# Attention and mixture of experts on one core: the first unit's heads spread in two chunks by SyncE, the second chunk's normalization on ScalarE, and the last tokens finished by pieces

## The chip, the core and the metric

The kernel runs on one core of a Trainium2 chip. The metric is the device time of the program in microseconds (us). Before the change it is 2261.02 us, the median of three runs (2259.83 to 2262.47). The profile comes from one further execution with the hardware profiler on.

## The reference, cut to what matters

x has 8 sequences of 1024 tokens with 256 values each, all in float32. There are 16 heads of 16 values and 8 experts of 512 hidden values.

```python
x = x + layernorm(attention(layernorm(x), Wq, Wk, Wv, Wo))   # causal softmax attention
x = x + layernorm(moe(layernorm(x), ...))
# moe: logits = h @ router_weight.T + router_bias; the two best of softmax(logits)
#      each chosen expert: gate, up = split(h @ gate_up_proj[e] + bias)
#      act = (clip(up, -7, 7) + 1) * min(gate, 7) * sigmoid(1.702 * min(gate, 7))
#      out = sum of the two of weight * (act @ down_proj[e] + down_bias[e])
```

## The kernel before, in words

**Attention** works in 32 units: unit u is a sequence b and a group g of four heads. The projections give q and k as [channel, token] in the tiles `unq` and `unk`. For a unit, `spread(u)` (L607) copies the 16 rows of each of its four heads to partitions 0, 32, 64 and 96 of `qP` and `kP`, with DMAs that SyncE (SP) issues: four for q and four for k, each of 16 rows and all 1024 tokens. For unit 0 alone the four for k are issued by ScalarE (ACT) (L615).

A unit is then done in steps (`STEPS`, L627 to L639). `maxima_tiles` computes scores `sa` (L686) and their row maxima on VectorE (DVE); in the next unit's time `values_tiles` computes the transposed scores `sb` (L781), their exponentials on ScalarE and the weighted values `av` (L818). The first two steps of a unit read only the first 512 tokens of `qP` and `kP`; the third and the fourth read the second 512.

Everything else (layer norms, projections of later units, the output projection, the router) is cut into small pieces by generators with hand-written costs. `pump` hands such pieces out between the pairs of heads. The order of TensorE (PE), DVE, ACT and SP in the attention part is the order of the source; GpSimd (POOL) keeps it by `in_order`.

**The beginning** (`begin`, L449) loads x and the weights, computes the layer norm statistics of the first sequence's two chunks of 512 tokens, and applies them in `apply` (L469): of the four rows of tiles `n` of a chunk, ACT does n = 0 and 2 (L481), DVE does n = 1 and 3 (L392). Then, for each chunk t, `turn_x` transposes the normalized tokens on PE (`xps`, L436) and ACT copies them (L437); `project_chunk` multiplies by the q and k weights (`pjq`, `pjk`, L591) and ACT copies into `unq`, `unk` (L595). At the end `begin` puts memsets on POOL: `mx`, the two `vpad` tiles, and `qP` and `kP` of units 1 and 2 (L510 to L515). POOL has nothing else to do there, so it starts on them as soon as the second `rstd` (L380) is done.

After `begin` comes `spread(0)`, then the generator `others` (L518). Its first step issues, all on SP, the loads of the router's weights `rwr` (L521), the biases `gubr` (L523), four broadcasts `rbias` (L525) and a store of zeros. Its next four steps transpose the v and o weights (`wps_v`, `wps_o`, L443) with copies on ACT (L444); these run ahead of the loop over units. The step after those is handed out by the first `pump` in unit 0: it transposes `rwr` (`rps`, L537), and the next one `gubr` (`gubps`, L541). So on PE the order is: `xps`, `pjq`, `pjk` of chunk 1; `wps_v`, `wps_o`; four matmuls `sa` of the first step's first pair of heads; `rps`; `gubps`; `sa` of the second pair; values `vps` (L577), and so on.

**The experts** work on 71 tiles of 256 rows sorted by expert. Each tile's results are scattered to `ytd` in DRAM by two indirect DMAs of POOL (L1337). `both(t)` (L1347) finishes 512 tokens: it loads the attention result (`x1`, L1350) and the two expert results of each token (`yy`, 1 MB, L1354), combines them with the router's weights (ACT L1368, DVE L1373), takes statistics (L1377, L1378), `ve` (L1381), `rstd` on POOL (L1385), `shift` (L1390), normalizes on ACT (L1397), adds `x1` on DVE (L1402) and stores 512 KB (L1404). It is a generator too; its steps are placed between the matmuls of later tiles by `an_end` (L1428). The 16th group of tokens is ready only when all tiles are done, so its `both` runs alone at the very end (L1468).

Of the kernel before, what the change touches and what calls it, by code (L numbers as in the profile page):

```python
# [13 lines left out]
ALU = mybir.AluOpType  # L14
# [44 lines left out]
def attn_moe_kernel(  # L59
# [345 lines left out]
    with ExitStack() as attn:  # L405
# [43 lines left out]
        def begin():  # L449

            wr = {}
            for name, w, queue, tag in (
                ("q", wq, nc.sync, "avs"), ("k", wk, nc.sync, "avs"),
                ("v", wv, nc.scalar, "aT"), ("o", wo, nc.scalar, "aT"),
            ):
                wr[name] = ap2.tile([P, KT, D], F32, tag=tag, name=f"wr_{name}")
                queue.dma_start(out=wr[name], in_=w.rearrange("(t p) i -> p t i", p=P))
            xt = xs[0]
            xnTs[0] = ap0.tile([P, KT, S], F32, tag="xnT", name="xnT_0")
            steps = [ln_steps(xt[:, ts(t, NTB), :], NTB) for t in range(NC)]  # L460

            def all_of(gen):
                while True:
                    try:
                        next(gen)
                    except StopIteration as end:
                        return end.value

            def apply(t, mv, rstd):  # L469
                shift = small.tile([P, NTB], F32, tag="shift", name="shift")  # L470
                nc.vector.scalar_tensor_tensor(
                    shift, mv[:, :, 0:1].rearrange("p n c -> p (n c)"), -1.0, rstd,
                    ALU.mult, ALU.mult,
                )
                xn = ap3.tile([P, NTB, D], F32, tag="xn", name=f"xn_0_{t}")
                for n in range(NTB):
                    of = xt[:, t * NTB + n, :]
                    if n % 2:
                        ln_apply(xn[:, n, :], of, mv, rstd, n)
                    else:  # L480
                        nc.scalar.activation(  # L481
                            xn[:, n, :], of, AF.Identity,
                            bias=shift[:, n : n + 1], scale=rstd[:, n : n + 1],
                        )
                return xn

            for name in ("q", "k"):
                uns[0, 0, name] = ap0.tile(
                    [P, S], F32, tag=f"un{name}0", name=f"un{name}_0_0"
                )  # L490
            fill(0)
            got = all_of(steps[0])
            for kt in range(KT):
                weights("q", wr["q"], kt)
            for _ in range(NTB // 2):
                next(steps[1])
            xn = apply(0, *got)
            got = all_of(steps[1])
            for kt in range(KT):
                weights("k", wr["k"], kt)  # L500
            for kt in range(KT):
                turn_x(0, 0, xn, kt)
            xn = apply(1, *got)
            for t in range(NC):
                if t:
                    for kt in range(KT):
                        turn_x(0, t, xn, kt)
                for name in ("q", "k"):
                    project_chunk(0, 0, name, t)
            for mx in mxs:  # L510
                in_order(nc.gpsimd.memset(mx, NEG))
            for vp in vps:
                in_order(nc.gpsimd.memset(vp, 1.0))
            for i in range(1, NU):
                fill(i)  # L515
            return wr
# [71 lines left out]
        def project_chunk(b, g2, name, c):  # L588
            ps = ps_b.tile([P, QC], F32, tag="b", name=f"pj{name}_{b}_{g2}_{c}")
            for kt in range(KT):  # L590
                nc.tensor.matmul(  # L591
                    ps, lhsT=wT[name][:, kt, ts(g2, P)], rhs=xnTs[b][:, kt, ts(c, QC)],
                    start=(kt == 0), stop=(kt == KT - 1),
                )
            nc.scalar.copy(uns[b, g2, name][:, ts(c, QC)], ps)  # L595
# [8 lines left out]
                    yield piece(pe=1.75, act=0.6, after=0 if c else 1)  # L604
                    project_chunk(b, g2, name, c)

        def spread(u):  # L607

            b, g = divmod(u, NG)
            row = qPs[u % NU].rearrange("(h r) (a n s) -> h r a n s", r=HS, n=TN, s=D)  # L610
            for a in range(S // (TN * D) if u >= NU else 0):
                nc.sync.dma_start(out=row[:, DH, a], in_=zeros[:HG, :, :D])
            for name, dsts in (("q", qPs), ("k", kPs)):

                queue = nc.scalar if u == 0 and name == "k" else nc.sync  # L615
                for hh in range(HG):
                    queue.dma_start(
                        out=dsts[u % NU][ds(hh * HS, DH), :],
                        in_=uns[b, g // 2, name][ds((g % 2 * HG + hh) * DH, DH), :],
                    )  # L620


# [508 lines left out]
        with tc.manual_schedule(  # L1131
# [2 lines left out]
            free[0] = False  # L1134
            jobs = {}
            wr = begin()
            spread(0)
            more = start(due, others(wr))
            for _ in range(2 * KT):
                emit(due, more)  # L1140
# [203 lines left out]
        yield  # L1344


    def both(t):  # L1347

        x1 = ap2.tile([P, NTB, D], F32, tag="y", name=f"x1_{t}")
        nc.sync.dma_start(out=x1, in_=x1_dram[t])  # L1350
        yy = x_buffer(f"yy_{t}")[:, : NTB * TOPK * D].rearrange(
            "p (n r d) -> p n r d", n=NTB, r=TOPK
        )
        load = nc.sync.dma_start(  # L1354
            out=yy,
            in_=yt_dram[ds(t * TB * TOPK, TB * TOPK), :].rearrange(
                "(p n r) d -> p n r d", p=P, n=NTB
            ),
        )
        ahead_of(load, "yt")  # L1360
        yield
        acc = ap2.tile([P, NTB, D], F32, tag="xT", name=f"acc_{t}")
        st = small.tile([P, NTB, 6], F32, tag="st", name="st")
        mv = small.tile([P, NTB, 2], F32, tag="mv", name="mv")

        for n in range(NTB + 1):
            if n < NTB:
# [9 lines left out]
                nc.vector.bn_stats(st[:, m, :], acc[:, m, :])  # L1377
                nc.vector.bn_aggr(mv[:, m, :], st[:, m, :])  # L1378
            yield
        ve = small.tile([P, NTB], F32, tag="ve", name="ve")  # L1380
        nc.vector.tensor_scalar(  # L1381
            ve, mv[:, :, 1:2].rearrange("p n c -> p (n c)"), EPS, None, ALU.add
        )
        rstd = small.tile([P, NTB], F32, tag="rstd", name="rstd")
        in_order(nc.gpsimd.tensor_tensor(rstd, ve, nhalf, ALU.pow))  # L1385
        yield
        yield

        shift = small.tile([P, NTB], F32, tag="shift", name="shift")
        nc.vector.scalar_tensor_tensor(  # L1390
            shift, mv[:, :, 0:1].rearrange("p n c -> p (n c)"), -1.0, rstd, ALU.mult, ALU.mult
        )
        yield
        o = ap2.tile([P, NTB, D], F32, tag="aT", name=f"o_{t}")
        for n in range(NTB + 1):
            if n < NTB:
                nc.scalar.activation(  # L1397
                    o[:, n, :], acc[:, n, :], AF.Identity,
                    bias=shift[:, n : n + 1], scale=rstd[:, n : n + 1],
                )  # L1400
            if n:
                nc.vector.tensor_tensor(o[:, n - 1, :], o[:, n - 1, :], x1[:, n - 1, :], ALU.add)  # L1402
            yield
        nc.sync.dma_start(out=out_t[t], in_=o)  # L1404

    def tiles_for(r):

# [5 lines left out]
    with tc.manual_schedule(engines={engines.PE, engines.DVE, engines.Activation}):  # L1413
# [52 lines left out]
        for _ in behind:  # L1466
            pass
        for r in [*waiting, *range(ready, NT)]:  # L1468
            ends.append((0, both(routed[r])))
        while ends:  # L1470
            an_end(NTILES)
        free[0] = True
# [36 lines left out]
```

## Time and profile before

| what | value |
|---|---|
| median of three runs | 2261.02 us (2259.83 to 2262.47) |
| the profiled execution's own time | 2283.45 us |
| its span in the trace | 2281.7 us |
| PE busy | 2197.9 us, 96% of the span |
| DVE busy | 1634.9 us, 72% |
| ACT busy | 1091.0 us, 48% |
| POOL busy | 1067.7 us, 47% |
| mean granted TensorE clock | 0.979 |

The span is the trace's first to last event; what lies around it is 1.75 us. A line of the timeline gives start, duration, engine, source line, operation, output and inputs, sizes and count, and in brackets how long the engine had been idle and what ended that. SPq and ACTq are the DMA-issuing sides of SyncE and ScalarE. A line of the windows gives, for a stretch of time, the busy time and the number of instructions of PE, its weight loads, DVE, ACT and POOL, then the granted TensorE clock (1.00 is full), the DMA engines' share and GB/s.

### The profile page before, as it was taken

Reading aid. Unit: us, or ns where it says so; the run is one execution under the profiler, and the core shown is the slowest. Engines: PE = TensorE matmul, PEld = TensorE weight load, DVE = VectorE, ACT = ScalarE, POOL = GpSimd, SP = SyncE. Lnnn points to the kernel's source line nnn. Section 1 sums busy time; section 2 is a strip of 40 time slices with the busy share of each in tenths; the row PEclk is TensorE's granted clock in tenths of the full one; section 3 lists DMA queues with packets and bytes.
Section 4 is the critical chain, followed back from the end, with each engine's and each line's share of the span. In section 5 each row is a group of like instructions: output and inputs, shape, how many; then the busy total and the mean of one; then the engine's idle time right before and its main releaser. Section 6 shows DMA issues by size and latency. Waiting matters only on the chain.

```text
span 2281.7 us, 45149 instructions
## 1 busy us (share of the span) xinstructions
PE 2197.9 (96%) x16801; PEld 1374.6 (60%) x16801; DVE 1634.9 (72%) x3677; ACT 1091.0 (48%) x2181; POOL 1067.7 (47%) x1228
## 2 busy tenths in 40 slices
PE   7999999999999999999999999799999999999995
PEld 4444444544445445445545444577888888888884
DVE  4766777777767767877767786375557888887775
ACT  2466665566666666666656656331212323332222
POOL 3321462572573463464473364355444544554543
PEclk8899999999999999999999999899999999999998
DMA  3101102102101111111111121458567877878773
GB/s 80 34 7 39 25 16 55 41 20 48 43 26 32 49 36 30 48 30 39 48 29 35 34 57 35 153 189 252 197 204 267 274 264 254 276 250 277 246 247 111
DMA packets 149106, 251.05 MB, mean 110 GB/s; under 512 B 25920, under 2 KB 111832, under 8 KB 146840
## 3 DMA queue, kind: packets, MB, share of 16 engines
q1 hardware_dynamic: 134168, 210.86, 30.2%
q0 software_dynamic: 12960, 35.47, 4.3%
q8 instruction: 133, 2.18, 0.4%
q10 hardware_dynamic: 1760, 1.84, 0.4%
q14 instruction: 85, 0.70, 0.1%
HBM read 175.66 MB, written 55.68 MB: 101 GB/s over the span
## 4 chain that ended last, share of the span: by engine, by line
PE 83%; POOL 6%; DVE 5%; issue 3%; ACT 1%; DMA 1%; SPq 0%; POOLq 0%; ACTq 0%; DVEq 0%
PE sa L686 19%; PE gu L1296 19%; PE av L818 11%; PE dn L1327 10%; PE sb L781 7%; PE vps L577 3%; PE pjk L591 3%; PE pjq L591 3%; PE yps L877 2%; PE avt L849 1%; PE xtps L1280 1%; POOL pT L798 1%; PE aps L869 1%; POOL xsd L1044 1%; POOL xn L392 1%
## 5 line engine op out<-in xcount | busy, mean ns | idle before, releaser
L789 ACT ACTIVATE pT<-sb 128x512 f32<-128x512 f32 x1152 | 625.0, 595 | 433.8 <-PE sb L781 381.3
L781 PE MATMUL sb<-qP,kP 32*128 32x512 f32 (+3 forms) x3072 | 722.1, 528 | 4.0 <-ACT pT L789 2.6
L686 PE MATMUL sa<-kP,qP 32*128 32x512 f32 (+3 forms) x3072 | 665.3, 532 | 3.5 <-DVE mx L702 2.2
L1296 PE MATMUL gu<-xsT,wg 128*128 128x256 f32 x2272 | 520.2, 382 | 1.2 <-ACT xsT L1282 1.2
L1296 PEld LDWEIGHTS gu<-xsT,wg 128*128 128x128 f32 x2272 | 434.0, 191 | 61.5 <-ACT xsT L1282 1.5
L798 POOL TENSOR_SCALAR_AFFINE_SELECT pT<-pT 128x512 f32<-128x512 f32 x256 | 159.5, 639 | 580.9 <-ACT pT L789 573.9
L702 DVE TENSOR_REDUCE mx<-sa 128x2 f32<-128x1024 f32 x256 | 311.8, 1219 | 127.9 <-PE sb L781 116.3
L1307 ACT ACTIVATE sig<-gate 128x256 f32<-128x256 f32 x284 | 118.3, 416 | 570.7 <-DVE gate L1305 523.7
L686 PEld LDWEIGHTS sa<-kP,qP 32*128 32x128 f32 x3072 | 232.7, 187 | 195.3 <-issue 101.0
L818 PE MATMUL av<-pT,vpad 128*32 128x256 f32 (+1 forms) x5120 | 348.5, 369 | 1.5 <-DVE avs L829 0.9
L1312 POOL TENSOR_TENSOR sig<-sig,gate 128x256 f32<-128x256 f32 x284 | 213.6, 753 | 291.2 <-ACT sig L1307 288.3
L781 PEld LDWEIGHTS sb<-qP,kP 32*128 32x128 f32 x3072 | 309.5, 186 | 44.7 <-ACT pT L789 15.7
L1327 PE MATMUL dn<-wd,act 128*128 128x256 f32 x1136 | 274.5, 382 | 16.4 <-DVE act L1317 16.4
L818 PEld LDWEIGHTS av<-pT,vpad 128*32 128x32 f32 x5120 | 116.8, 109 | 286.4 <-issue 216.7
L1305 DVE TENSOR_SCALAR gate<-gu,bs 128x256 f32<-128x256 f32 x284 | 135.9, 479 | 168.0 <-PE gu L1296 148.8
L1327 PEld LDWEIGHTS dn<-wd,act 128*128 128x128 f32 x1136 | 209.5, 191 | 48.8 <-DVE act L1317 23.7
L696 DVE CUSTOM_DVE_ANT_0 sa<-sa,cmask 128x512 f32<-128x512 f32 x256 | 178.2, 698 | 61.8 <-PE sb L781 30.6
L1337 POOL DMA_INDIRECT ytd<-ys,places x142 | 142.8, 1006 | 125.0 <-DVE ys L1333 98.5
L1044 POOL DMA_INDIRECT xsd<-xn,slots x128 | 127.5, 996 | 95.9 <-DMA xn<-second 51.4
L1317 DVE SCALAR_TENSOR_TENSOR act<-up,sig 128x256 f32<-128x256 f32 x284 | 124.4, 438 | 24.9 <-POOL sig L1312 24.9
L711 DVE TENSOR_REDUCE mx<-sa 128x2 f32<-128x512 f32 x128 | 87.9, 687 | 72.1 <-PE sb L781 42.6
L1309 DVE TENSOR_SCALAR up<-gu,bs 128x256 f32<-128x256 f32 x284 | 134.7, 474 | 0.0
(198 smaller groups left out, 2395.0 us busy)
## 6 DMA issues: line engine op xcount, KB each, us to landing
wg<-_L_ffn_gate_up_proj_dram SPq DMA_DIRECT2D x71, 1024.0 KB
wd<-in_L_ffn_down_proj_dram SPq DMA_DIRECT2D x71, 512.0 KB
xs<-xsd SPq DMA_DIRECT2D x67, 257.0 KB
yy<-ytd SPq DMA_DIRECT2D x16, 1024.0 KB
bs<-biasd SPq DMA_DIRECT2D x71, 132.0 KB
x<-in_L_attn_x_dram SPq DMA_DIRECT2D x16, 512.0 KB
qP<-unq SPq DMA_DIRECT2D x128, 64.0 KB
x1d<-y SPq DMA_DIRECT2D x16, 512.0 KB
```

Source lines behind the costliest of these rows:

```text
L686: nc.tensor.matmul(ps[:, hh, ds(at, w)], lhsT=qP[r, ts(i, P)], rhs=kP[r, ds(c * QC, w)], start=True, stop=True,)
L696: nc.vector.tensor_tensor_reduce(out=ps[:, hh, :], in0=ps[:, hh, :], in1=cmask, scale=1.0, scalar=NEG, op0=ALU.add, op1=ALU.max, accum_out ...
L702: nc.vector.tensor_reduce(mx[:, heads, i, 2:3], ps, AX.X, ALU.max)
L781: nc.tensor.matmul(banks[hh][:, ds(at, QC - off)], lhsT=kP[r, ts(j, P)], rhs=qP[r, ds(c * QC + off, QC - off)], start=True, stop=True,)
L789: nc.scalar.activation(pT[:, 2 * pair + hh, :], banks[hh], AF.Exp)
L798: in_order(nc.gpsimd.affine_select(out=d, in_=d, compare_op=ALU.is_ge, fill=0.0, base=0, pattern=[[0, HG], [1, P]], channel_multiplier=-1,))
L818: nc.tensor.matmul(av[ds(hh * HS, HS), ds(off + a - at, z - a)], lhsT=vp[:, j, ds((g * HG + hh) * VS, HS)], rhs=pT[:, hh, a:z],  start=c n ...
L1044: put = nc.gpsimd.indirect_dma_start(out=xs_dram[:, :], out_offset=bass.IndirectOffsetOnAxis(ap=slots[:, t, r, n : n + 1], axis=0), in_=xn ...
L1296: nc.tensor.matmul(ps[:, half, :], lhsT=wg[:, kt, ds(half * FF + f * P, P)], rhs=xT[:, kt, :], start=(kt == 0), stop=(kt == KT - 1),)
L1312: in_order(nc.gpsimd.tensor_tensor(sg, sg, gt, ALU.mult))
L1327: nc.tensor.matmul(ps[:, n, :], lhsT=act[:, f, ts(n, P)], rhs=wd[:, f, :], start=(f == 0), stop=(f == FT - 1),)
L1337: put = nc.gpsimd.indirect_dma_start(out=yt_dram[:, :], out_offset=bass.IndirectOffsetOnAxis(ap=places[:, i, n : n + 1], axis=0), in_=y[:, ...
```

## The change

Four edits at two places.

1. In `apply`, DVE normalizes rows n = 1 and 3 only for chunk 0; for chunk 1 ACT does all four.
2. `spread` gets a range of tokens, `cols`. `begin` calls it for unit 0 after each chunk's projections with that chunk's 512 tokens, so unit 0 takes 16 DMAs of half the size in place of 8, all issued by SP; ACT issues none. The call after `begin` is gone, so the loads of `others` stand on SP behind all 16.
3. `both` for the last 512 tokens (`final`) loads `yy` by four DMAs, one for each n, and no longer takes part in the ordering exception `ahead_of`, which lets later scatters pass a load.
4. In that `both`, `ve`, `rstd`, `shift`, the normalization, the addition and the store are done for two rows at a time. For all other tokens one piece of four remains, in the order of before.

```diff
                 for n in range(NTB):
                     of = xt[:, t * NTB + n, :]
-                    if n % 2:
+                    if n % 2 and t == 0:
                         ln_apply(xn[:, n, :], of, mv, rstd, n)
...
                 for name in ("q", "k"):
                     project_chunk(0, 0, name, t)
+                spread(0, ts(t, QC))
...
-        def spread(u):
+        def spread(u, cols=slice(0, S)):
...
-                queue = nc.scalar if u == 0 and name == "k" else nc.sync
                 for hh in range(HG):
-                    queue.dma_start(
-                        out=dsts[u % NU][ds(hh * HS, DH), :],
-                        in_=uns[b, g // 2, name][ds((g % 2 * HG + hh) * DH, DH), :],
+                    nc.sync.dma_start(
+                        out=dsts[u % NU][ds(hh * HS, DH), cols],
+                        in_=uns[b, g // 2, name][ds((g % 2 * HG + hh) * DH, DH), cols],
                     )
...
             wr = begin()
-            spread(0)
...
-    def both(t):
+    def both(t, final=False):
...
+        if final:
+            for n in range(NTB):
+                nc.sync.dma_start(out=yy[:, n], in_=of[:, n])
+        else:
+            ahead_of(nc.sync.dma_start(out=yy, in_=of), "yt")
...
+        size = NTB // 2 if final else NTB
         for n in range(NTB + 1):
...
             yield
+            if n and n % size == 0:
+                g = slice(n - size, n)
+                nc.vector.tensor_scalar(
+                    ve[:, g], mv[:, g, 1:2].rearrange("p n c -> p (n c)"), EPS, None, ALU.add
+                )
+                in_order(nc.gpsimd.tensor_tensor(rstd[:, g], ve[:, g], nhalf[:, g], ALU.pow))
         yield
         yield
         o = ap2.tile([P, NTB, D], F32, tag="aT", name=f"o_{t}")
+        for g in (slice(a, a + size) for a in range(0, NTB, size)):
+            nc.vector.scalar_tensor_tensor(
+                shift[:, g], mv[:, g, 0:1].rearrange("p n c -> p (n c)"), -1.0, rstd[:, g],
+                ALU.mult, ALU.mult,
+            )
             yield
+            for n in range(g.start, g.stop + 1):
+                if n < g.stop:
+                    nc.scalar.activation(o[:, n, :], acc[:, n, :], AF.Identity, ...)
+                if n > g.start:
+                    nc.vector.tensor_tensor(
+                        o[:, n - 1, :], o[:, n - 1, :], x1[:, n - 1, :], ALU.add
+                    )
+                yield
+            nc.sync.dma_start(out=out_t[t][:, g], in_=o[:, g])
...
-            ends.append((0, both(routed[r])))
+            ends.append((0, both(routed[r], r == NT - 1)))
```

More of the change, by code (lines that the diff above doesn't have):

```diff
@@ L1353, in both @@
         )
[L1354 to L1358, printed above, removed]
-        )
-        ahead_of(load, "yt")
+        of = yt_dram[ds(t * TB * TOPK, TB * TOPK), :].rearrange(
+            "(p n r) d -> p n r d", p=P, n=NTB
+        )
+        if final:
[3 more added lines that the diff above has]
+            ahead_of(nc.sync.dma_start(out=yy, in_=of), "yt")
         yield
@@ L1364, in both @@
         mv = small.tile([P, NTB, 2], F32, tag="mv", name="mv")
+        ve = small.tile([P, NTB], F32, tag="ve", name="ve")
+        rstd = small.tile([P, NTB], F32, tag="rstd", name="rstd")
+        shift = small.tile([P, NTB], F32, tag="shift", name="shift")
+        size = NTB // 2 if final else NTB
         for n in range(NTB + 1):
@@ L1379, in both @@
             yield
[L1380 to L1385, printed above, removed]
+            if n and n % size == 0:
[4 more added lines that the diff above has]
+                in_order(nc.gpsimd.tensor_tensor(rstd[:, g], ve[:, g], nhalf[:, g], ALU.pow))
         yield
         yield
[L1389 to L1393, printed above, removed]
-        o = ap2.tile([P, NTB, D], F32, tag="aT", name=f"o_{t}")
[L1395 to L1402, printed above, removed]
-            yield
-        nc.sync.dma_start(out=out_t[t], in_=o)
+        o = ap2.tile([P, NTB, D], F32, tag="aT", name=f"o_{t}")
+        for g in (slice(a, a + size) for a in range(0, NTB, size)):
[3 more added lines that the diff above has]
+            )
+            yield
+            for n in range(g.start, g.stop + 1):
+                if n < g.stop:
+                    nc.scalar.activation(
+                        o[:, n, :], acc[:, n, :], AF.Identity,
+                        bias=shift[:, n : n + 1], scale=rstd[:, n : n + 1],
+                    )
+                if n > g.start:
+                    nc.vector.tensor_tensor(
+                        o[:, n - 1, :], o[:, n - 1, :], x1[:, n - 1, :], ALU.add
+                    )
+                yield
+            nc.sync.dma_start(out=out_t[t][:, g], in_=o[:, g])
     def tiles_for(r):
```

## The prediction

> **What bounds the kernel now.** I read the page first (busy shares and the chain that ended last), then the timeline of the first 45 us and of the last 30, then the clock by windows. The chain is TensorE's for the greatest part, so work saved on other engines counts only where PE waits for them.
>
> ```profile
> PE 83%; POOL 6%; DVE 5%; issue 3%; ACT 1%; DMA 1%; SPq 0%; POOLq 0%; ACTq 0%; DVEq 0%
> ```
>
> The change touches two such places. The first is the beginning:
>
> ```profile
> 12.80 8.07 DVE L392 TENSOR_SCALAR xn<-x,mv,rstd 128x256 f32<-128x256 f32 x2
> 12.87 3.96 POOL L513 MEMSET vpad<- 128x2296 f32 x2
> 13.09 1.09 ACT L481 ACTIVATE xn<-x,shift,rstd 128x256 f32<-128x256 f32 x2
> 16.36 0.27 PE L436 MATMUL xps<-ident,xn 128*128 128x128 f32 x1
> 19.46 0.95 POOL L431 MEMSET kP<- 128x1024 f32 x1
> 20.61 1.76 PE L436 MATMUL xps<-ident,xn 128*128 128x128 f32 x7 [3.98 <-DVE xn L392]
> 25.52 2.54 SPq L617 DMA_DIRECT2D qP<-unq  x4
> 27.18 2.52 ACTq L617 DMA_DIRECT2D kP<-unk  x4
> 28.11 0.53 SPq L521 DMA_DIRECT2D rwr<-L_ffn_router_weight_dram  x1
> 30.19 0.58 PE L443 MATMUL wps_o<-ident,wr_o 128*128 128x128 f32 x2 [2.54 <-ACT wvT L444]
> 30.70 2.46 PE L686 MATMUL sa<-kP,qP 32*128 32x512 f32 x4
> 32.56 0.32 PE L537 MATMUL rps<-ident,rwr 8*128 8x8 f32 x2
> ```
>
> See that DVE's two rows of chunk 1 take from 12.80 to 20.87, which is as long as POOL's memsets run, and that PE stands still for 3.98 us because of it. Later PE waits 2.54 us more: ACT can't copy `wvT` while it issues the DMAs of k.
>
> Each of these pauses is followed by a halved clock (third column from the right; after the stretch come PE's busy time and count):
>
> ```profile
> 20.20:23.60 3.40, 2.99 (x9) 2.17 (x10) 0.67 (x2) 1.17 (x2) 0.21 (x1) 0.51 0.00 0
> 30.40:33.80 3.40, 3.40 (x11) 1.93 (x11) 0.48 (x1) 0.67 (x3) 0.00 (x0) 0.50 0.17 28
> 40.60:44.00 3.40, 3.40 (x9) 2.35 (x8) 0.69 (x1) 0.59 (x1) 0.00 (x0) 0.50 0.53 125
> ```
>
> The second place is the end, where nothing runs beside the last tokens:
>
> ```profile
> 2260.32 0.96 POOL L1337 DMA_INDIRECT ytd<-ys,places  x1 [0.30 <-issue]
> 2263.71 0.32 SPq L1354 DMA_DIRECT2D yy<-ytd  x1
> 2268.52 1.70 ACT L1368 ACTIVATE acc<-yy,chosen_w 128x256 f32<-128x256 f32 x4 [12.75 <-DMA yy<-ytd]
> ...
> 2273.40 0.17 DVE L1381 TENSOR_SCALAR ve<-mv 128x4 f32<-128x4 f32 x1
> 2273.66 1.04 POOL L1385 TENSOR_TENSOR rstd<-ve,nhalf 128x4 f32<-128x4 f32 x1 [12.38 <-DVE ve L1381]
> 2274.93 2.07 ACT L1397 ACTIVATE o<-acc,shift,rstd 128x256 f32<-128x256 f32 x4 [4.71 <-DVE shift L1390]
> 2277.49 0.39 SPq L1404 DMA_DIRECT2D out_dram<-o  x1
> ```
>
> See the serial chain: scatter, whole load (4.81 us), combining, `rstd`, normalizing, whole store, end at 2281.7.
>
> **What the Trainium skill says.** "SBUF — State Buffer", section "Who interferes with whom": a VectorE tensor_scalar in a two-port mode and a GpSimd instruction exclude each other for whole instructions, and ScalarE waits on nobody. The trace agrees: the same two rows of chunk 0 took 0.73 us (9.05), those of chunk 1 8.07 us beside memsets, ACT's beside the same memsets 1.09 us. "TensorE: Matmul & The Clock Gate", section "What's actually happening": after an idle window of about 3.4 us the clock is halved, and a busy one restores it. The trace agrees in the main (0.99 before 20.2, 0.51 after, 1.00 from 23.6), but from 30.4 to 44.0 PE was busy throughout and still at 0.50. "DMA: Bandwidth & Descriptors", section "Issuing engines are not separate DMA queues": a second issuing engine saves only the time of issuing. Here that time is 2.5 us for four DMAs, and it counts.
>
> **Part 1, chunk 1 on ACT: the stall of 3.98 us goes.** ACT does four rows in place of two: 2 x 0.545 more, from 13.09 to 15.2. Behind them on ACT stands the copy `unq` of chunk 0, which could start at 14.84; it moves to 15.2 and ends at 15.8. The next, `unk`, waits for PE until 16.56 anyway, so the extra 1.1 us are covered by PE's `pjk` (14.64 to 16.52). What is late next: PE goes from `pjk` into all eight `xps` at about 16.5, ACT copies at 17.2 and 17.85, and `pjq` starts at about 17.85 (before 22.19). I take the pace of chunk 0, 4.16 us from the start of `pjq` (12.40) to the copy of `unk` (16.56): `unk` is copied from 22.0 to 22.6 (before 26.57 to 27.16), 4.6 us earlier. DVE's freed time is worth nothing; its next work was at 33.32.
>
> **Part 2, spread.** SP issues 16 DMAs in place of 4 here. Each takes 2.54 / 4 = 0.635 us; halving the bytes should not change the price of issuing. SP can start when `unq` of chunk 0 is there, at 15.85; that wait holds only the DMAs behind it, which start no earlier before. 16 x 0.635 = 10.2 us: SP is busy to 26.0, with no wait on the way (chunk 1's q come up at 20.9, its k at 23.5, after their copies at about 20.9 and 22.6). ACT, rid of 2.52 us, copies `wvT` at 22.6; `wps_o` runs at about 23.0 and `sa` could start at 23.4. Its k of chunk 0 is issued from 18.4 to 20.9 and lands some 2.0 to 2.6 us after an issue begins (a wait for `xn` at 1310.59 and one for `qP` at 799.61, both told by the chain), so `sa` isn't held.
>
> But `rwr` and `gubr` stand behind all 16 on SP: issued at 26.05 and 26.65 (before 28.11 and 28.69), landing at about 28.4 and 29.1. PE reaches `rps` after four `sa` at 24.5 and **waits there some 4 us**. So `gubps` ends at about 29.4, where before it ended at 33.46. Of nearly 9 us PE is ahead, **4.0 us** remain. SP, not PE, sets this sum: 12 more issues at 0.635 on it. Everything behind on SP (`rbias`, zeros, `spread(1)` at 32.72) also comes some 2 us earlier; unit 1 needs it only after 66.
>
> From there to 65 PE was busy in nearly every window, so the lead stays. The new pause costs the full clock again, as the old one did: at half speed from about 27 to 30 on, for as long as before (13.6 us) in the likeliest case. With windows at the old phase PE would leave it at 40.6, having done 0.5 us more slow work than before: -0.3. **Net 3.7 us.**
>
> **Part 3, loading by pieces.** The loads go out at 2263.71 and then every 0.54 us (2226.59 to 2227.13 on SP). The first quarter lands about 2.5 us after its issue, the others by 2268.5, since 1 MB moves at the same speed. Neither is shown before: bounds are 2.05 us (`xn` above) and 4.0, if small rows are slow. DVE needs 1.05 us a row (2269.06 to 2270.14). So: 2266.2 + 0.54 (ACT) + 4 x 1.05 + 0.3 for two `ve` = 2271.25, where before `ve` ended at 2273.57: **2.3 us** (bounds 0.8 to 2.8). Dropping `ahead_of` here costs nothing, since no scatter follows.
>
> **Part 4, two halves.** The first half's `rstd` lies beside the second's statistics. Then `shift` 0.2, ACT 1.1, an addition 0.45 end the first half at 2273.1; its additions stand ahead of the second `shift` on DVE: 0.2 + 1.1 + 0.5 more, store at 2274.9. Before: 2277.49. So 0.3 us beyond part 3. The last store has half the bytes; the data of the whole one ran about 1.5 us (2278.4 to 2280.2 in the DMA row), so about 0.7 less (bounds 0 to 0.9). **Parts 3 and 4: 3.3 us** (bounds 1.0 to 4.0).
>
> **Sum.** 3.7 + 3.3 = 7.0 us of the profiled execution's 2283.45 us (span 2281.7), 0.31%. The median shown is 2261.02, 1% less; in proportion that gives 2254.0 us.
>
> **The rivals.**
> - *Both leads and a shorter slow spell.* In 20.2 to 23.6 one busy window was enough to restore the clock. If a window falls well on `vps`, PE leaves the spell some 6.8 us sooner, worth half: 3.3 us more, 2250.7. For it: the first spell; against: two others of 13.4 to 13.6 us (30.4 and 67.9).
> - *A longer slow spell.* If the spell starts only at 30.4 and lasts 13.6 us, 4.5 us more of work is slow, at a price of 2.2 us: 2256.2.
> - *The early lead is lost,* because a later wait on SP's loads or on DVE holds PE at its old time. Then only the end counts: 3.3 us, 2257.7. Against it: PE without gaps from 30.7 to 54.5.
> - *Slower: SP's issues cost more than 0.635 us,* because each of 16 small transfers waits for an earlier one to land (SP did so once, 0.8 us ahead of L525). `rps` is then late, and PE has nothing else to do. Against the gain at the end and `rps` at 32.56 this decides from about 1.1 us an issue ((32.56 + 3.3 - 2.4 - 15.85) / 16); at 1.9 us `rwr` is issued at 46.2, `rps` comes at 48.6, 16 us late, less 3.3: 2273.6. Against it: the groups of four seen here took 2.43 to 3.01 us, 0.61 to 0.75 each.
> - *The last tokens aren't taken by the new path:* excluded by L1409, which gives 71 for r = 15 with 71 tiles.
>
> **How the numbers follow.** Likeliest 0.55 (2254.0, own range 2251.5 to 2256), shorter spell 0.20, longer 0.10, lead lost 0.10, slower 0.05. A measurement of this kernel can tell about 0.2%, 4.5 us: faster is below 2256.5. The first two and 0.06 of the third lie there: 0.81; the rest of the third and the fourth are the same, 0.14; slower 0.05. The range takes in the shorter spell with a good end and the lost lead with a poor one: 2248 to 2259.
>
> **What would show it.** Right: no POOL-long row of DVE at 12.8; `xps` without a pause at 16.5; `unk` of chunk 1 by 23; 16 DMAs on SP from 15.9 to 26; PE idle ahead of `rps` for about 4 us; `gubps` done near 29.4; at the end the first `acc` some 2.5 us after the first `yy` load, and the last store 2.6 us earlier. Wrong: SP's 16 issues well beyond 10 us, `sa` held until chunk 1's transfers land, pieces that land together, or a clock that stays at half far beyond 44.

## The result, and the profile after

| what | before | after |
|---|---|---|
| median of 8 runs each | 2260.16 us (2253.48 to 2263.2) | 2250.68 us (2249.65 to 2256.47) |
| ratio of the times | | 0.9964 [0.9952, 0.9976] |
| the profiled execution's own time | 2283.45 us | 2251.17 us |
| its span | 2281.7 us | 2249.5 us |
| PE busy / PE idle in that span | 2197.9 / 83.8 us | 2174.3 / 75.2 us |
| mean granted TensorE clock | 0.979 | 0.989 |

The kernel is faster by 9.5 us, 0.36%, with an interval that lies wholly below 1. Two later comparisons of the same two kernels gave 0.9994 [0.9982, 1.0006] and 0.9965 [0.9947, 0.9983], so the size of the gain depends on when it is measured; that is taken up below.

The two profiled spans are 32.2 us apart, far more than the medians. The page shows why this must not be read as the gain. Here are the busy shares and the chain by engine of the kernel after:

```profile
PE 2174.3 (97%) x16801; PEld 1362.3 (61%) x16801; DVE 1623.0 (72%) x3677; ACT 1092.4 (49%) x2183; POOL 1067.2 (47%) x1229
PE 87%; DVE 5%; POOL 3%; issue 2%; ACT 2%; DMA 1%; SPq 0%; ACTq 0%; DVEq 0%; POOLq 0%
```

The change takes no matmul away, yet PE's busy time is 23.6 us smaller (2197.9 - 2174.3). That is the clock: what a span loses by it is (1 - 0.979) x 2281.7 = 47.9 us before and (1 - 0.989) x 2249.5 = 24.7 us after, which differ by 23.2 us. Only 8.6 us of the 32.2 are PE's idle time. A further profile of the unchanged kernel (the first experiment below) had a span of 2253.7 us and 2175.6 us of PE. So most of the 32.2 us belongs to the one execution of before that was profiled.

Now the beginning, in the timeline of the kernel after. The lines answer to those from 12.8 on that the prediction showed:

```profile
13.24 3.96 POOL L515 MEMSET vpad<- 128x2296 f32 x2
13.48 2.07 ACT L482 ACTIVATE xn<-x,shift,rstd 128x256 f32<-128x256 f32 x4
16.41 2.54 SPq L617 DMA_DIRECT2D qP<-unq  x4
17.26 1.04 PE L436 MATMUL xps<-ident,xn 128*128 128x128 f32 x8
19.06 2.42 SPq L617 DMA_DIRECT2D kP<-unk  x4
21.57 2.43 SPq L617 DMA_DIRECT2D qP<-unq  x4
22.32 0.58 ACT L597 COPY unk<-pjk 128x512 f32<-128x512 f32 x1 [1.13 <-PE pjk L593]
23.62 1.13 PE L686 MATMUL sa<-kP,qP 32*128 32x512 f32 x4
24.10 2.43 SPq L617 DMA_DIRECT2D kP<-unk  x4
26.57 0.53 SPq L523 DMA_DIRECT2D rwr<-L_ffn_router_weight_dram  x1
28.44 0.35 PE L539 MATMUL rps<-ident,rwr 8*128 8x8 f32 x2 [3.70 <-DMA rwr<-L_ffn_router_weight_dram]
29.42 0.34 PE L543 MATMUL gubps<-ident,gubr 64*128 64x64 f32 x1 [0.63 <-DMA gubr<-_L_ffn_gate_up_bias_dram]
29.69 2.08 PE L686 MATMUL sa<-kP,qP 32*128 32x512 f32 x4
```

DVE's row of 8 us is gone, ACT's four rows take 2.07 us beside the memsets, and all eight `xps` run without a pause. SP issues its 16 DMAs without a break from 16.41 to 26.53. The four `sa` run at once, at 23.62, and then PE stands still for 3.70 us, and for 0.63 us more: the router's weights are issued only behind the 16 DMAs. In the end PE reaches the second `sa` at 29.69, where before it did so at 33.39.

The clock windows of the kernel after, the same stretches and columns as in the prediction:

```profile
23.60:27.00 3.40, 1.14 (x5) 0.30 (x4) 1.51 (x4) 0.51 (x2) 0.00 (x0) 1.00 0.23 51
27.00:30.40 3.40, 1.33 (x5) 0.96 (x7) 0.58 (x3) 0.00 (x0) 0.00 (x0) 0.70 0.12 23
30.40:33.80 3.40, 3.40 (x9) 1.75 (x6) 1.52 (x4) 0.00 (x0) 0.00 (x0) 0.50 0.13 32
33.80:37.20 3.40, 3.40 (x16) 2.03 (x16) 0.69 (x1) 0.59 (x1) 0.00 (x0) 0.80 1.07 203
37.20:40.60 3.40, 3.40 (x28) 2.51 (x27) 1.10 (x3) 1.54 (x3) 0.00 (x0) 1.00 0.60 74
```

The new pause costs the full clock too, but only for some 7 us, two windows in place of the four that the profiled execution of before had. As a sum: (1 - 0.70 + 0.50 + 0.20) x 3.4 = 3.4 us of full-speed work are lost here; before, 4 x 0.5 x 3.4 = 6.8 us were.

The end of the kernel after, same view:

```profile
2230.49 0.96 POOL L1336 DMA_INDIRECT ytd<-ys,places  x1 [0.30 <-issue]
2233.87 1.74 SPq L1359 DMA_DIRECT2D yy<-ytd  x4
2237.61 0.51 ACT L1373 ACTIVATE acc<-yy,chosen_w 128x256 f32<-128x256 f32 x1 [11.68 <-DMA yy<-ytd]
2238.31 0.51 ACT L1373 ACTIVATE acc<-yy,chosen_w 128x256 f32<-128x256 f32 x1 [0.19 <-DMA yy<-ytd]
2238.98 1.13 ACT L1373 ACTIVATE acc<-yy,chosen_w 128x256 f32<-128x256 f32 x2 [0.16 <-DMA yy<-ytd]
2240.42 0.17 DVE L1387 TENSOR_SCALAR ve<-mv 128x2 f32<-128x2 f32 x1
2242.76 0.17 DVE L1387 TENSOR_SCALAR ve<-mv 128x2 f32<-128x2 f32 x1
2243.65 0.92 DVE L1408 TENSOR_TENSOR o<-o,x 128x256 f32<-128x256 f32 x2 [0.67 <-ACT o L1403]
2244.49 0.15 DVE L1396 SCALAR_TENSOR_TENSOR shift<-mv,rstd 128x2 f32<-128x2 f32 x1
2244.60 2.04 SPq L1412 DMA_DIRECT2D out_dram<-o  x2
2245.31 0.92 DVE L1408 TENSOR_TENSOR o<-o,x 128x256 f32<-128x256 f32 x2 [0.67 <-ACT o L1403]
```

The four loads do go out one after the other, but the first of them is usable only 3.74 us after its issue (2233.87 to 2237.61), and the next ones about 0.7 us apart. From the first load to the end of the span it is 15.6 us, where before it was 18.0. The second half's `shift` waits behind the first half's additions, as the prediction had it.

### The profile page after: what moved, and what is told of

Read it like the earlier page. It is cut to its first block, busy times and chain, and to the rows that moved or that the text cites. A ratio compares the mean times of both kernels' runs of the same rounds, so it can differ in the third digit from the quotient of the medians.

```text
span 2249.5 us, 45170 instructions
## 1 busy us (share of the span) xinstructions
PE 2174.3 (97%) x16801; PEld 1362.3 (61%) x16801; DVE 1623.0 (72%) x3677; ACT 1092.4 (49%) x2183; POOL 1067.2 (47%) x1229
## 4 chain that ended last, share of the span: by engine, by line
PE 87%; DVE 5%; POOL 3%; issue 2%; ACT 2%; DMA 1%; SPq 0%; ACTq 0%; DVEq 0%; POOLq 0%
PE sa L686 21%; PE gu L1295 19%; PE av L818 12%; PE dn L1326 10%; PE sb L781 8%; PE vps L579 3%; PE yps L877 3%; PE pjk L593 3%; PE pjq L593 3%; PE avt L849 1%; PE xtps L1279 1%; PE aps L869 1%; ACT pT L789 1%; PE xps L436 1%; PE x2ps L935 1%
## 5 line engine op out<-in xcount | busy, mean ns | idle before, releaser
L686 PE MATMUL sa<-kP,qP 32*128 32x512 f32 (+3 forms) x3072 | 657.5, 526 | 3.3 <-DVE mx L702 2.9
L1326 PEld LDWEIGHTS dn<-wd,act 128*128 128x128 f32 x1136 | 209.4, 191 | 50.8 <-DVE act L1316 25.8
```

What stands on the lines that cost most here:

```text
L686: nc.tensor.matmul(ps[:, hh, ds(at, w)], lhsT=qP[r, ts(i, P)], rhs=kP[r, ds(c * QC, w)], start=True, stop=True,)
L1326: nc.tensor.matmul(ps[:, n, :], lhsT=act[:, f, ts(n, P)], rhs=wd[:, f, :], start=(f == 0), stop=(f == FT - 1),)
```

## The experiments

The theory is that of the prediction: one stall of PE is removed, a wait for the router's weights takes part of that back, and the last tokens' chain becomes shorter. The rivals: that one of the edits does all or nothing; that the wait isn't due to SP's queue; and that what differs is only the clock.

Three figures are read from every profile: when the **second `sa`** of unit 0 starts (the beginning is over there), the **end length** from the issue of the first `yy` load to the end of the span, and PE's idle time, which is the span less PE busy. In the table the ratio is to the kernel before, run in the same session. There were three sessions, of four rows each; "before there" is the median of the kernel before in that session.

| run | median us (n) | before there, us (n) | ratio | second sa, us | end length, us | PE idle, us |
|---|---|---|---|---|---|---|
| before, again | 2256.52 (12) | 2253.77 (59) | 1.0006 [0.9991, 1.0022] | 33.47 | 17.95 | 78.1 |
| edit 1 alone | 2251.7 (14) | 2253.77 | 0.999 [0.9978, 1.0003] | 28.77 | 18.1 | 74.3 |
| edit 2 alone | 2257.32 (22) | 2253.77 | 1.0015 [1.0005, 1.0025] | 34.44 | 17.9 | 79.3 |
| edits 3 and 4 alone | 2250.4 (22) | 2253.77 | 0.999 [0.9981, 0.9999] | 27.79 | 14.9 | 71.1 |
| after, again | 2253.34 (14) | 2255.24 (42) | 0.9994 [0.9982, 1.0006] | 28.98 | 15.7 | 74.3 |
| router loads first | 2245.77 (6) | 2255.24 | 0.9954 [0.9938, 0.9969] | 23.77 | 15.5 | 68.0 |
| edits 1, 3, 4 | 2249.04 (13) | 2255.24 | 0.9974 [0.9962, 0.9986] | 27.39 | 15.0 | 71.0 |
| before, memsets behind | 2251.52 (22) | 2255.24 | 0.9984 [0.9974, 0.9994] | 27.52 | 18.2 | 73.1 |
| after, a third time | 2267.25 (9) | 2275.26 (17) | 0.9965 [0.9947, 0.9983] | 29.13 | 15.1 | 77.7 |
| one queue, not chunked | 2265.79 (6) | 2275.26 | 0.9946 [0.9928, 0.9965] | 29.05 | 15.6 | 76.2 |
| pieces of the load only | 2267.47 (9) | 2275.26 | 0.9963 [0.9946, 0.998] | 28.82 | 16.8 | 78.3 |
| router loads first, again | 2262.69 (6) | 2275.26 | 0.9927 [0.9907, 0.9946] | 24.32 | 15.2 | 74.8 |

The last session (from "after, a third time" on) was slower for every kernel, the kernel before among them (2275.26 us), so rows of different sessions are compared only by their ratios and by the three figures.

### The kernel before, profiled again

No edit.

> The kernel before, profiled again, to learn what of the 32 us between the two profiled spans belongs to the change. Theory: the time between the start of one sequence and the next was 175.0 us in the first profile of before and 172.4 in that of after because of a pause at each sequence's boundary that only this one execution had; here the span should be about 2259 us (the median of the timed runs less what lies around it) and the distance 172.4 to 172.8. The stall of 3.98 us ahead of the chunk 1 transposes, the first scores at 30.7 and the end of the bias transpose at 33.5 should be as in the first profile within 0.5 us. Rival: the pause belongs to the kernel before, the distance is 175.0 again, and most of what the change gains is gained there.

Measured: a span of 2253.7 us with clock 0.987, in place of 2281.7 us with 0.979. The stall is there again, in the timeline of this run:

```profile
12.87 8.07 DVE L392 TENSOR_SCALAR xn<-x,mv,rstd 128x256 f32<-128x256 f32 x2
20.68 1.75 PE L436 MATMUL xps<-ident,xn 128*128 128x128 f32 x7 [4.25 <-DVE xn L392]
```

What follows: the stall and the end (17.95 us against 18.0) repeat to a few tenths, while the rest of the span moves by 28 us between two executions of one kernel. The theory holds: from the first `xps` of one sequence to that of the next it is 172.5 to 174.0 us here for the last four sequences, 174.9 to 175.7 in the first profile and 172.5 to 172.9 in that of the kernel after. The longer distance belongs to one execution and not to the kernel. The slow clock after the second pause lasted two windows here, not four; after the first pause it lasted two, not one, so that the first scores came at 32.05 and not at 30.7 as expected. The two places, second `sa` and end length, are worth more than the two spans.

### Edit 1 alone: the second chunk's normalization on ACT

```diff
-                    if n % 2:
+                    if n % 2 and t == 0:
```

> Edit 1 alone: ACT normalizes all four rows of chunk 1, everything else is as before. Theory: the transposes of chunk 1 follow at 16.5 without a pause, k is copied by 22.6, ACT issues its four DMAs until 25.2, PE waits for wvT for some 2.8 us, scores start near 26.2 and the bias transpose ends near 28 to 29: 4.6 to 5.5 us ahead of before, so the time falls by 4 to 6 us, as much as the whole beginning is worth in the full change. Rival (edit 2 is needed for the lead to stay): PE is caught again by the wait for wvT and the lead at the bias transpose is 2 us or less.

Measured: 2251.7 us, 0.999 [0.9978, 1.0003], 2.1 us less in the medians with an interval that reaches no change. In its timeline PE goes into `xps` without a pause, and what waits next is the old wait for `wvT`:

```profile
16.93 1.04 PE L436 MATMUL xps<-ident,xn 128*128 128x128 f32 x8
25.61 0.69 PE L443 MATMUL wps_o<-ident,wr_o 128*128 128x128 f32 x2 [2.54 <-ACT wvT L444]
```

What follows: the edit does remove the stall, and the second `sa` comes 4.6 us ahead of before (33.39 to 28.77). `unk` of chunk 1 is copied at 21.99, before at 26.57: 4.6 us, which is the lead that the prediction's part 1 had worked out. In time only 2.1 us are seen, less than the 4 to 6 expected, and the interval (0.7 us slower to 5.0 us faster) holds both the 4.6 and no gain at all. The fourth experiment shows one thing that would make it smaller.

### Edit 2 alone: unit 0 spread by chunks, all on SP

```diff
                 for name in ("q", "k"):
                     project_chunk(0, 0, name, t)
+                spread(0, ts(t, QC))
...
-        def spread(u):
+        def spread(u, cols=slice(0, S)):
...
-            spread(0)
```

with the body of `spread` as in the change.

> Edit 2 alone: unit 0 spread by chunks, all 16 DMAs on SP, VectorE's rows as before. Theory: the stall of 4 us stays, k of chunk 1 is copied at 27.2, SP ends its 16 DMAs at 30.6, the router's weights land at 33, so PE waits for them and the bias transpose ends at 33.5 to 34.5; the time is that of before within 1 us, or up to 1 us longer. Rival (freeing ACT of its DMAs is what the beginning gains): scores start at 28 and the bias transpose ends by 31, 2.5 us faster.

Measured: 2257.32 us, 1.0015 [1.0005, 1.0025]: slower by 3.5 us in the medians. Its timeline has both waits at once:

```profile
20.54 1.75 PE L436 MATMUL xps<-ident,xn 128*128 128x128 f32 x7 [4.32 <-DVE xn L392]
31.53 0.53 SPq L522 DMA_DIRECT2D rwr<-L_ffn_router_weight_dram  x1
33.34 0.35 PE L538 MATMUL rps<-ident,rwr 8*128 8x8 f32 x2 [3.05 <-DMA rwr<-L_ffn_router_weight_dram]
```

What follows: the wait for `rwr` comes with edit 2 and needs nothing of edit 1. By itself edit 2 loses: PE is rid of the 2.54 us for `wvT`, and waits 3.05 and 0.49 us instead. The second `sa` comes 1.0 us later than before, as expected; the time is 3.5 us longer (1.1 to 5.6 by the ratio), where at most 1 us had been expected. What makes up the rest isn't shown.

### Edits 3 and 4 alone: the last tokens by pieces

The end as in the change, the beginning as before:

```diff
+        if final:
+            for n in range(NTB):
+                nc.sync.dma_start(out=yy[:, n], in_=of[:, n])
...
+        size = NTB // 2 if final else NTB
...
-            ends.append((0, both(routed[r])))
+            ends.append((0, both(routed[r], r == NT - 1)))
```

> Edits 3 and 4 alone: only the last tokens are taken by pieces. Theory: from the issue of the last load to the end of the span 15.6 us in place of 18.0, so 2.4 us faster, and nothing changes at the beginning. Rival (the pieces gain only by chance or their extra issues eat it): within 0.5 us of before.

Measured: 2250.4 us, 0.999 [0.9981, 0.9999], 3.4 us less in the medians; end length 14.9 us in place of 18.0. The surprise is at its beginning, whose code is that of before. Its timeline:

```profile
12.64 4.32 DVE L392 TENSOR_SCALAR xn<-x,mv,rstd 128x256 f32<-128x256 f32 x2
17.02 0.77 PE L436 MATMUL xps<-ident,xn 128*128 128x128 f32 x5 [0.18 <-DVE xn L392]
```

What follows: in this execution DVE's two rows took 4.32 us, not 8.07. They ended at 16.96 and PE waited 0.18 us, not 4. Taken one by one, each row lasted as long as one `vpad` memset here (2.23 and 2.17 us; the memsets 2.01 and 2.15). In the other three profiles with DVE in this place (before, before again, edit 2 alone) the first row alone took 7.75 us and ended only when all six memsets had. So **the stall of before isn't in every execution**, and in those where it is missing edit 1 has no such stall to remove. The end works by itself, with no help from the beginning. Whether it matters that the last load is out of `ahead_of` was not tried apart.

### The change, profiled again

No edit against the kernel after. It was run in each of the two later sessions.

> The whole change again, on the same chip as the three kernels beside it. Theory: its gain is edit 1's plus edits 3 and 4's, less about 1 us for edit 2: 3 to 6 us faster than before, with PE waiting some 4 us for the router's weights at about 24.7. The gain of edit 1 varies, because before doesn't lose its 4 us in each execution (in one execution with the old beginning VectorE's two rows took 4.3 us in place of 8.1, and PE waited 0.2 us). Rival (the parts work only together): 8 us or more, as first measured.

> The whole change a third time, to settle how much of the first result (9.5 us) and of the second (1.9 us) is the change. Theory: the change itself is worth some 1.5 us at the start (over before without its stall) to 6 us (with it) and 2.4 us at the end; single executions differ by several us because each slow spell of the clock is a whole number of 3.4 us windows. So 2 to 8 us faster than before, nearest 5. Rival (the first result was chance): within 2 us.

Measured: 2253.34 us against 2255.24, and 2267.25 us against 2275.26. The waits repeat: 3.93 and 0.70 us in the first of these profiles, 3.62 and 0.68 us in the second, after 3.70 and 0.63 us. The second `sa` came at 28.98 and 29.13, the end lengths were 15.7 and 15.1 us.

What follows: all that the change does by its code is the same in three profiles, but its gain in time was 9.5, 1.9 and 8.0 us. The second of these can't be told from no change and lies below the 3 to 6 us expected; the third is at the top of the 2 to 8 expected.

### The change with the router's loads first

```diff
                 queue.dma_start(out=wr[name], in_=w.rearrange("(t p) i -> p t i", p=P))
+            wr["r"] = ap2.tile([E, D], F32, tag="xT", name="rwr")
+            nc.sync.dma_start(out=wr["r"], in_=router_w)
+            wr["gub"] = ap2.tile([E * 2 * FT, P], F32, tag="xT", name="gubr")
+            nc.sync.dma_start(out=wr["gub"], in_=gate_up_b.rearrange("e (c p) -> (e c) p", p=P))
...
-            rwr = ap2.tile([E, D], F32, tag="xT", name="rwr")
-            nc.sync.dma_start(out=rwr, in_=router_w)
-            gubr = ap2.tile([E * 2 * FT, P], F32, tag="xT", name="gubr")
-            nc.sync.dma_start(out=gubr, in_=gate_up_b.rearrange("e (c p) -> (e c) p", p=P))
+            rwr, gubr = wr["r"], wr["gub"]
```

> The change, with the loads of the router's weights and biases issued in the beginning, ahead of unit 0's 16 DMAs on SP. Theory: the wait at rps is the price of edit 2 and goes: scores at 23.6, the bias transpose ends by 25.5 in place of 29.8, PE has no pause over 2 us after 9, so the slow clock from 28 to 35 goes too: 4.4 to 7.8 us faster than the change itself. Rival (PE then waits for chunk 1's transfers instead, or the slow clock comes anyway): less than 2 us faster than the change.

> The change with the router's loads first, again beside the change on one chip. Theory: 4 to 8 us faster than the change, 8 to 12 us faster than before, the bias transpose ending by 25.5 to 24. Rival (its lead on the other chip was the clock's phase): less than 3 us faster than the change.

Measured: 2245.77 us and 2262.69 us, 0.9954 [0.9938, 0.9969] and 0.9927 [0.9907, 0.9946] of before; beside the change of the same session that is 7.6 and 4.6 us less (5.0 to 10.4 and 0.4 to 12.0, when the recorded times of both kernels are drawn again at random). The timeline of the first one:

```profile
20.82 2.43 SPq L618 DMA_DIRECT2D qP<-unq  x4
22.45 1.13 PE L687 MATMUL sa<-kP,qP 32*128 32x512 f32 x4
23.41 0.23 PE L540 MATMUL rps<-ident,rwr 8*128 8x8 f32 x2
23.57 0.27 PE L544 MATMUL gubps<-ident,gubr 64*128 64x64 f32 x1
23.77 1.13 PE L687 MATMUL sa<-kP,qP 32*128 32x512 f32 x4
```

What follows: the same 16 DMAs are on the same queue; only two loads have been moved ahead of them, to 3.02 and 3.57 us. The wait is gone and PE runs on. So SP's queue in front of `rwr` was the cause. The spread's data was not: `sa` never waited for it. The second `sa` comes 5.2 and 4.8 us earlier than in the change's own run of the same session. The clock too stays at 1.00 through all windows from 16.8 to 50.8 in this profile; from `xps` to 40.0 PE has no pause of over 0.3 us. This version beats both kernels.

### Edits 1, 3 and 4, without edit 2

The kernel after, with `spread` as before:

```diff
-                spread(0, ts(t, QC))
...
+                queue = nc.scalar if u == 0 and name == "k" else nc.sync
...
-                    nc.sync.dma_start(
+                    queue.dma_start(
...
             wr = begin()
+            spread(0)
```

> Edits 1, 3 and 4 without edit 2: unit 0 is spread after both chunks, q by SP, k by ACT, as before. Theory: edit 2 gains nothing at the start, since PE waits for wvT (2.5 us) here and for the router's weights (3.7 and 0.6 us) there; the bias transpose ends near 28.8 here and near 29.7 there, so this is 0 to 2 us faster than the change. Rival (edit 2 carries the early lead): 2 us or more slower than the change.

Measured: 2249.04 us, 0.9974 [0.9962, 0.9986], 6.2 us less than before. The change ran at 2253.34 us in the same session. The waits of PE from 12 to 48 us (a line names who waits, for what, the sum, the count and the longest):

```profile
PE wps_o L443 <- ACT wvT L444: 2.5, 1, 2.5
PE pjq L592 <- ACT xnT L437: 0.3, 1, 0.3
PE wps_o L443 <- ACT unk L596: 0.2, 1, 0.2
```

What follows: without edit 2 PE waits 2.5 us for `wvT`; with it, 4.3 us for the router's loads. The second `sa` comes at 27.39, ahead of the change's three (28.98 to 29.69). Edit 1 alone, which has the very same beginning, had it at 28.77, since its slow clock fell earlier (0.66 in the window from 23.6 to 27.0, here 1.00). **Edit 2 takes away part of what the others gain**: 0.2 to 2.3 us by the place of the second `sa`, and 4.3 us in the medians, more than the 0 to 2 expected. When the recorded times of both kernels are drawn again at random, the 4.3 us become 1.3 to 6.4. With the run of edit 2 alone that makes two comparisons in which edit 2 loses; how much, they don't tell closely.

### Before, with the memsets held behind DVE's rows

```diff
                     project_chunk(0, 0, name, t)
+            seen = small.tile([P, 1], F32, tag="seen", name="seen")
+            in_order(nc.gpsimd.tensor_copy(seen, xn[:, NTB - 1, D - 1 : D]))
             for mx in mxs:
```

POOL reads one value of the last normalized row before its memsets, so they can't run beside these rows. Nothing is moved to ACT.

> Before, with one small copy on POOL that reads the last row of chunk 1's normalized tokens, put ahead of the memsets, so that POOL starts them only when VectorE's rows are done; nothing moves to ACT. Theory (the memsets keep VectorE out): the two rows take 0.7 to 0.8 us, the transposes of chunk 1 follow without a pause near 16.4, and the time is that of edit 1 alone, 2 to 5 us under before; and this holds in each execution. Rival (the rows are slow for another reason, such as their inputs): they still take 4 us or more.

Measured: 2251.52 us, 0.9984 [0.9974, 0.9994]. The timeline:

```profile
13.09 0.73 DVE L392 TENSOR_SCALAR xn<-x,mv,rstd 128x256 f32<-128x256 f32 x2
14.26 3.96 POOL L515 MEMSET vpad<- 128x2296 f32 x2
16.32 1.04 PE L436 MATMUL xps<-ident,xn 128*128 128x128 f32 x8
```

What follows: with the memsets out of the way DVE's rows take 0.73 us, as in chunk 0. That shows that POOL's memsets were the cause, and not DVE's own work or a late input. "SBUF — State Buffer", section "Who interferes with whom", of the Trainium skill gives the mechanism: the two engines share a port pair, and whoever has it keeps the other out for a whole instruction. The trace agrees, but for the length: DVE was kept out for six instructions on end. The stall is worth 3.7 us in the medians [1.4 to 5.9, from the ratio], though the second `sa` comes 5.9 us earlier than in the two profiles of before. A stall that is in some executions only, by the fourth experiment, would fit that; how often it is there was not counted.

### The change, on one queue but not by chunks

```diff
-                spread(0, ts(t, QC))
...
             wr = begin()
+            spread(0)
```

against the kernel after: eight DMAs of whole rows on SP after both chunks.

> The change with unit 0 spread after both chunks, in 8 whole DMAs, all on SP. Theory: what edit 2 costs is the queue, not the chunks: the first DMAs go out near 20.7 and SP ends them near 25.7, scores start near 25.5 to 26.5 in place of 22.6 to 23.6, but the router's weights are issued at 25.7 as in the change and land at the same time, so the bias transpose ends within 0.6 us of the change's and the time is the change's within 2 us. Rival (the early first chunk carries a lead): 3 us or more slower than the change.

Measured: 2265.79 us, beside 2267.25 us for the change. The timeline:

```profile
23.63 2.42 SPq L616 DMA_DIRECT2D kP<-unk  x4
26.04 1.70 PE L685 MATMUL sa<-kP,qP 32*128 32x512 f32 x4 [2.65 <-DMA kP<-unk]
28.22 0.32 PE L538 MATMUL rps<-ident,rwr 8*128 8x8 f32 x2 [0.48 <-DMA rwr<-L_ffn_router_weight_dram]
29.05 2.08 PE L685 MATMUL sa<-kP,qP 32*128 32x512 f32 x4
```

What follows: now `sa` waits for k, and `rps` hardly at all; the second `sa` comes at 29.05, as with chunks at 29.13. Spreading by chunks does bring the first `sa` forward, but its lead ends at the router's loads, which SP issues at 26.1 in both kernels. Four DMAs take 2.42 to 2.54 us here with 64 KB each, and as long with 32 KB each in the change: half the bytes cost the same to issue.

### The change, with the load by pieces but one half less

```diff
-        size = NTB // 2 if final else NTB
+        size = NTB
```

> The change with the last yy still loaded by four DMAs, but ve, rstd, shift, normalization, addition and store for all four rows at once. Theory: from the issue of the first yy load to the end of the span 18.0 us in before and 15.6 to 15.8 in the change; loading by pieces brings 0.8 to 1.1 of it (first quarter 3.7 us after its issue in place of 4.8 for the whole), so 16.9 to 17.2 here. Rival (the pieces of the load bring it all): 15.6 to 16.0.

Measured: 2267.47 us, beside 2267.25 us for the change; end length 16.8 us, between 18.0 and 15.1, and just under the 16.9 to 17.2 expected. The timeline of its end:

```profile
2248.89 1.74 SPq L1359 DMA_DIRECT2D yy<-ytd  x4
2252.67 0.51 ACT L1373 ACTIVATE acc<-yy,chosen_w 128x256 f32<-128x256 f32 x1 [11.73 <-DMA yy<-ytd]
2257.60 0.17 DVE L1387 TENSOR_SCALAR ve<-mv 128x4 f32<-128x4 f32 x1
2261.68 0.39 SPq L1412 DMA_DIRECT2D out_dram<-o  x1
```

What follows: the pieces of the load alone shorten the end by 1.2 us (18.0 - 16.8), and the halves with the smaller last store by 1.2 to 1.7 us more. How much of the halves' share is the earlier work and how much the smaller last store was not tried apart. In the medians one microsecond can't be seen.

## Why the prediction was right

The forecast was 2254.0 us, faster, in a range of 2248 to 2259. The median is 2250.68 us: the direction held, and the gain was 9.5 us in place of 7.0. By its steps:

- **Part 1, the stall.** Right. `unk` of chunk 1 was to be copied from 22.0 to 22.6 and was copied from 22.32 to 22.90. That it came so close has luck in it: all of this execution's beginning was some 0.4 us later (PE's first matmul `wps_q` at 8.88, before 8.49), PE came to the eight `xps` at 17.26 and not at 16.5 (`pjq` of chunk 0 took 2.92 us, before 2.41), and from `pjq` to `unk` it then took 3.74 us in place of the 4.16 taken from chunk 0. The two errors nearly cancel. Not foreseen was that the stall is missing in some executions of before (4.32 us in place of 8.07 for DVE's rows). The whole sum was made against a profile that had it.
- **Part 2, SP's queue.** Right, step by step: 16 DMAs in 10.2 us, measured 10.1; a wait of some 4 us ahead of `rps`, measured 3.70 and 0.63 us for the next; `gubps` done at 29.4, measured 29.76. Here too two errors cancel: `rwr` was issued at 26.57 and not at 26.05, and was usable 1.87 us after that and not 2.35. The net lead was to be 4.0 us, and the second `sa` came 3.7 us earlier. The rival by which each issue would cost 1.1 us or more fell: they cost 0.61 to 0.64. What the prediction didn't say is that edit 2 by itself loses; its own numbers had it (4.6 us of lead from part 1, 4.0 with part 2).
- **The clock after the new pause.** The likeliest case took a slow spell as long as before, 13.6 us, at a price of 0.3 us. It lasted 7 us, as in the rival at 2250.7 us. But two windows were also what the unchanged kernel had in its second profile (0.90, 0.50 and 0.59 in the windows from 30.4 to 40.6, the same loss of 3.4 us), so this isn't shown to be a gain of the change. The long spell belonged to one execution. That the time met the rival's number may be chance.
- **Parts 3 and 4, the end.** The mechanism is right, the size was too high: 3.3 us forecast, 2.4 us in this profile. In eight profiles with these edits the end length is 14.9 to 15.7 us, 15.3 on average; in five with the old end it is 17.9 to 18.2, 18.0 on average: 2.7 us. The term that was off is "the first quarter lands about 2.5 us after its issue". It took 3.74 us (3.0 to 3.8 over the profiles), near the bound of 4.0. Nor were the others there by 4.8 us after the first issue: ACT took up the third after 5.11. It may be that the piece shares the DMA engines with the three behind it; that wasn't tested. So `ve` ended 9.06 us after the issue, before 9.86: 0.8 us in place of 2.3, which is the low bound that was kept for this. The halves gave more than foreseen: from the last `ve` to the last store's issue 3.92 us before, 3.3 after (0.6 in place of 0.3); from there to the end 4.2 before, about 3.25 after (0.95 in place of 0.7). Sum: 0.8 + 0.6 + 0.95 = 2.4 us.
- **The sum.** 3.7 us at the beginning and 2.4 at the end are 6.1 us as read from the traces, near the 7.0 forecast. The medians gave 9.5, 1.9 and 8.0 us in three comparisons. The 6.1 us are shown by the experiments; what the medians have beyond or short of them isn't, and the median's nearness to the forecast owes something to chance: the gain of the second comparison would have put it at 2259.1 us.

**What stays open.** Why the gain varies so between the comparisons. The record narrows it down. Take from each span the time up to the second `sa` and the end length: what is left, in which no edit changes the code, is 2202.3 to 2207.3 us in nine of the ten profiles of the first result and of the first two sessions, with the change and without it. It is 2230.3 us in the first profile of before, and 2218.9 to 2226.0 in the last session. So what moves spans by 20 to 30 us lies where the change touches nothing, and it shows as 9 to 24 us more of PE busy. Its cause isn't known.

Three things are seen that would move the gain by a few microseconds. The stall is missing in some executions of before. The number of slow clock windows differs from one execution to the next, also of one kernel (from 61 to 75 us the change's first profile has the clock at 0.72, 0.50, 0.50 and 0.78 in four windows; the run without edit 2 has 0.57, 0.50 and 0.92 in three), and each full slow window costs 1.7 us of work (3.4 x 0.5). And the mean clock of the timed runs was the same for both kernels in the second comparison (0.9860 after, 0.9861 before), but not in the third (0.9846 and 0.9824). By an estimate from these figures that is 0.0022 x 2270 = 5 us of the 6.1 us by which the two gains differ; whether the change had a part in it isn't shown. How often the stall is there wasn't counted, since only one execution of a run is profiled. Edit 2 costs 3.5 and 4.3 us in the medians, where the second `sa` shows 0.2 to 2.3 us; the medians' intervals (1.1 to 5.6 and 1.3 to 6.4 us) are so wide that the two need not disagree.

## What to carry to other kernels

Before a queue is given more DMAs, look at what stands behind them: the issues cost some 0.63 us each, with 64 KB as with 32 KB, and a load that needs nothing from the work in front of it belongs ahead of it, as the two loads of the router show, which were worth 4.6 to 7.6 us. When a change of a few microseconds is judged, read the places in the trace (start of the next step, length of the tail) and profile the unchanged kernel twice; one pair of spans differed here by 32 us, of which the change explains about 6. A transfer that is cut in pieces doesn't give its first piece after a quarter of the time.

## What the runs showed of the hardware that was not expected

- **Cutting a load.** 1 MB loaded by one DMA was usable 4.8 us after its issue. The first of four pieces of 256 KB, issued one behind the other, took 3.0 to 3.8 us. In the kernel after, ACT took up the third only 5.1 us after the first issue (2238.98), later than the whole load of before.
- **DVE beside a series of POOL's memsets** waits with one row for the whole series of six in three executions, and in a fourth loses one memset with each row: 8.07 against 4.32 us for the same two rows, at the same place. With the memsets behind them it was 0.73 us.
- **The clock.** "TensorE: Matmul & The Clock Gate", section "What's actually happening", of the Trainium skill has the full clock back after at least one busy window of about 3.4 us. Of the length the traces agree: the slow spells last 6.83 us in the kernel after (28.35 to 35.18), 13.65 in the first profile of before (30.35 to 44.00) and 20.48 with the router's loads first (52.81 to 73.30), which are two, four and six times 3.41. Of the busy window they don't: in the last of these PE was busy for all of each of the six windows, and the clock stayed at half. One stretch of it:

```profile
55.80:59.20 3.40, 3.40 (x14) 1.29 (x12) 2.42 (x3) 0.00 (x0) 0.00 (x0) 0.50 0.00 0
```

This spell came after a pause of PE of only 1.19 us (50.38 to 51.57), about a third of a window; a pause of 1.15 us ahead of 41.22 in the same profile was followed by the full clock. So a slow spell can begin after a pause far shorter than a window, and busy windows alone don't end it. What does, was not tried.
